# Last group's low parts by TensorE, in two named PSUM banks: an edge-gated graph layer

## The chip, the cores and the metric

The kernel runs on one core of a Trainium2 chip. The time is the device time of one execution in microseconds (us); the kernel before has a median of 1105.02 us over 3 runs (1098.43 to 1110.40). The engines are TensorE (PE, with its weight loads as PEld), VectorE (DVE), ScalarE (ACT), GpSimd (POOL) and SyncE (SP). Each works through its own instructions in order, and semaphores tie them together.

## The reference

The inputs are `x` (16 batches, 1024 nodes, 256 features) and one sparse adjacency matrix `adj` (1024 x 1024, about 9 entries in a row). For every batch, cut to what matters:

```python
pre_u = einsum('bud,dk->buk', h, W1[:d])
pre_v = einsum('bvd,dk->bvk', h, W1[d:])
hidden = relu(pre_u[:, :, None, :] + pre_v[:, None, :, :] + b1)
S = sigmoid(einsum('buvk,ko->buvo', hidden, W2)[..., 0] + b2[0])
a = einsum('buv,bud->bvd', S * A, h)
m = einsum('uv,bud->bvd', A, h) * h
z = beta1*h + beta2*(a @ Wa + ba) + beta3*(m @ Wm + bm)
```

The gate `S` is wanted only where `adj` is not zero, so the kernel works on a list of edges. Each edge (u, v) needs `pre_u` of u, `pre_v` of v, and `h` of u.

## The kernel before, in words

**Blocks, tiles, edges.** The 16 batches make four groups `g` of four. The 1024 receiving nodes make eight blocks `vt` of 128. A step `k` is one block of one group, 32 in all; the last eight (k = 24 to 31) are the last group. A block has ten tiles `n`, two windows of 64 nodes with five tiles each; a tile is 128 edges. Position `s` is a tile's place (0 to 9) in its block.

**Tables.** For each group a table in HBM holds, for each node u, `pre_u` and `h` of the four batches (2048 numbers). Its first half is made by `rows` (line 452), its second is copied. A tile fetches 128 rows of it by an indirect gather (`fetch`, line 515, on POOL) into one of eight `fetched` buffers.

**pre_v as two parts.** `pre_v` plus `b1` of a block is computed by `halves` (line 473) in two halves of 512 columns (two batches each): one matmul puts down the row `b1` (`add_row`, line 448), and `half_product` (line 442) adds the product with `w_v`. The sum is then spread to edges by a 0/1 matrix `mark` in a matmul. That matmul works in the shorter type float32r, so the sum is kept as two numbers: its rounded value, and the low part, which is the sum minus the rounded value. The tile `X` has two windows of 128 rows: in window 0 rows 0 to 63 hold the rounded values of nodes 0 to 63 and rows 64 to 127 their low parts; in window 1 rows 64 to 127 hold the rounded values of nodes 64 to 127 and rows 0 to 63 their low parts. ACT moves the parts there 64 rows at a time. One matmul over 128 rows so adds the rounded value and the low part of 64 nodes. In `halves` ACT casts the product to `X` (line 482) and copies it whole to `low` (line 483), DVE subtracts the rounded value from `low` for both halves at once (line 484), and ACT copies the parts to their places (lines 486 and 489).

**One tile.** `expand` (line 602, PE) makes `pc`, `pre_v` of each edge, in one of two PSUM buffers of 1024 columns. `add` (line 637, DVE) adds it to the fetched `pre_u`. `gate` (line 641) has four DVE instructions that take the relu, multiply by `W2` and sum to a score for each batch, then ACT's sigmoid (line 650) and four ACT instructions that scale the selection matrix `left` (line 652). `aggregate` (line 655, PE) multiplies `left` with the fetched `h` and sums into `acc`.

**One block's end.** ACT copies `acc` to `ev` (`half_end`), PE transposes it in `turn_over` (line 674) into a small PSUM tile, ACT copies that to `LT` (line 685), DVE multiplies by `h` (line 696), and `block_end` (line 701) makes the output product: a bias row, then products with `w_a` and `w_m`, which ACT copies (line 718) and DVE adds to `h` (line 719).

**Banks.** All small products (`pre_v`, transposes, output products, the table's rows) live in a PSUM pool of two banks, handed out in turn by `small` (line 220). A new tile waits until the bank's former tile has been read.

**Order.** The order of the engines' instructions is written out by hand: the loop at line 860 emits, for each tile n, the aggregates of earlier tiles (at odd n, two tiles together), `add(n + 1)`, `gate(n)`, delayed work (`do`), `expand(n + 2)`, and then `products` (line 800). From the tenth tile on, `products` places the work on the block before and the block after by position: transposes at s = 8, 9, 0 and 2, the two halves of the next block's `pre_v` at s = 1 and 3, and the output products at s = 4 to 7. The subtraction of `low` is emitted at s = 5, after the gate, two tiles after the second half; ACT's three moves into `X` come at s = 4, 6 and 7. The first expansion that reads the new `X` is at s = 8.

Of the kernel before, what the change touches and what calls it, by code (L numbers as in the profile page):

```python
# [7 lines left out]
FP = mybir.dt.float32  # L8
FR = mybir.dt.float32r
I32 = mybir.dt.int32  # L10
AF = mybir.ActivationFunctionType
ALU = mybir.AluOpType
AX = mybir.AxisListType
P = 128
# [3 lines left out]
def kernel(  # L18
# [42 lines left out]
    nc = tc.nc  # L61
    B, N, D = x.shape
    NT = N // P
    DC = D // P
    GB = 4
    NG = B // GB
    GD = GB * D
    W = 64
    NW = P // W
# [24 lines left out]
    def load_weights(src, name, engine=nc.scalar):  # L94
        t = const.tile([P, DC, D], FP, name=name)
        engine.dma_start(t, src.rearrange("(c p) k -> p c k", p=P))
        return t
# [3 lines left out]
    def fixed(shape, name, dt=FP):  # L101
        return const.tile(shape, dt, name=name)
# [9 lines left out]
    upto = fixed([P, E], "upto")  # L112
# [3 lines left out]
    row = rows32[:, 0:1]  # L116
# [43 lines left out]
    same = hv.rearrange("p w q one -> p (w q) one").to_broadcast([P, NW * Q, V])  # L160
# [12 lines left out]
    slot_of = fixed([P, NW, TW], "slot_of")  # L173
    for w in range(NW):
        nc.vector.tensor_scalar(slot_of[:, w, :], upto[:, :TW], float(P), row, ALU.mult, ALU.add)
    ident = fixed([P, P], "ident")
    nc.vector.tensor_scalar(ident, upto[:, :P], row, None, ALU.is_equal)
    place = upto[:, :W].rearrange("p (q v) -> p q v", v=V)
    slot, nth = upto, upto[:, :S]

# [11 lines left out]
    b1_p = fixed([P, D], "b1_p", FR)  # L192
# [13 lines left out]
    main = ctx.enter_context(ExitStack())  # L206
    gat = main.enter_context(tc.tile_pool(name="gat", bufs=1))
    one = main.enter_context(tc.tile_pool(name="one", bufs=1))
    big = main.enter_context(tc.tile_pool(name="big", bufs=2))
# [5 lines left out]
    lst = lst.enter_context(tc.tile_pool(name="lst", bufs=1))  # L215
    psc = main.enter_context(tc.tile_pool(name="psc", bufs=2, space=bass.MemoryType.PSUM))
    psa = main.enter_context(tc.tile_pool(name="psa", bufs=1, space=bass.MemoryType.PSUM))
    psm = main.enter_context(tc.tile_pool(name="psm", bufs=2, space=bass.MemoryType.PSUM))

    def small(name):  # L220
        return psm.tile([P, 512], FP, name="misc")


    def aside(vt):
# [177 lines left out]
    def after(step, f):  # L402
        due.setdefault(step, []).append(f)
# [5 lines left out]
    order = [(g, vt) for some in (range(FIRST), range(FIRST, NT)) for g in range(2) for vt in some]  # L409
    again = [(g, vt) for g, vt in order if vt >= FIRST or g == 1]  # L410
    order += [(g, vt) for g in range(2, NG) for vt in range(NT)]
    hTs = {}
# [29 lines left out]
    def half_product(p, hT, wt, h, begun):  # L442
        for bb in range(2):
            for i in range(DC):
                nc.tensor.matmul(p[:, bb * D:(bb + 1) * D], hT[:, 2 * h + bb, i, :], wt[:, i, :],  # L445
                                 start=(i == 0 and not begun), stop=(i == DC - 1), skip_group_check=begun)

    def add_row(p, parts):
        nc.tensor.matmul(p, unit, parts.unsqueeze(1).to_broadcast([P, 2, D]),  # L449
                         start=True, stop=False, skip_group_check=True)  # L450
# [19 lines left out]

    cuts = {}

    def halves(k):
        X = cuts[k] = big.tile([P, NW, GD], FR, name="X")
        low = one.tile([P, GD], FP, name="low")
        for h in range(2):
            step = yield
            c = slice(2 * h * D, (2 * h + 2) * D)
            p = small("p")
            add_row(p, b1_p)  # L480
            half_product(p, hTs[order[k]], w_v, h, True)
            nc.scalar.copy(X[:, 0, c], p)
            nc.scalar.copy(low[:, c], p)  # L483
        after(step + (2 if k else 1), lambda: nc.vector.tensor_tensor(low, low, X[:, 0, :].bitcast(FP), ALU.subtract))  # L484
        yield
        nc.scalar.copy(X[W:, 1, :], X[W:, 0, :].bitcast(FP))
        for w in range(NW):
            yield
            nc.scalar.copy(X[(1 - w) * W:(2 - w) * W, w, :], low[w * W:(w + 1) * W])
# [5 lines left out]
    def do(step):  # L495
        for f in due.pop(step, ()):
            f()

    def go(gen, step):

        try:
            gen.send(step)
        except StopIteration:
            pass

    T = TW * NW

    BS = NG * NT
# [25 lines left out]
    w_v = load_weights(W1[D:2 * D], "w_v", nc.sync)  # L534
# [11 lines left out]
    marks, pcs, accs, evs, hbs, LTs, lefts = {}, {}, {}, {}, {}, {}, {}  # L546
# [12 lines left out]
    parts = halves(0)  # L559
# [76 lines left out]

    def add(n):
        t = fetched[at_slot[n]][:, :GD]
        nc.vector.tensor_tensor(t, t, pcs.pop(n), ALU.add)  # L639

    def gate(n):
        m = len(QUARTERS[n % TW])
# [157 lines left out]
    def products(n, k, s):  # L800
        nonlocal end, parts
        made_rows(n)
        if (s == 2 and 0 < k < BS) or n == total:
            turn_over(k - 1, 1, 1, n)
        z = 3 if n < ROOM else 4
        if z <= s < z + 4 and 0 < k < BS:
            if s == z:
                end = block_end(k - 1)
                next(end)
            go(end, n)  # L810
        if ROOM <= n < total - T:
            if s in (8, 9):
                turn_over(k, 0, s - 8, n)
        elif s == 7 and k < BS:
            turn_over(k, 0, 0, n)
        if s == 7 and k == BS - 1 or s == 8 and n < ROOM:
            turn_over(k, 0, 1, n)
        if (s == 0 and 0 < k < BS) or n == total - 1:
            turn_over(k - (s == 0), 1, 0, n)
        if n == total - 2:  # L820
            end = tail(tails[:2], n)
            next(end)
        elif n == total - 1:
            go(end, n)
        elif n >= total:
            end = tail([tails[2 + n - total]], n)
            next(end)
            go(end, n)
            go(end, n)
        later = n >= ROOM  # L830
        if k + 1 < BS and s - later in (0, 2, 3, 5, 6):
            if s == later:
                parts = halves(k + 1)
                next(parts)
            go(parts, n)

# [22 lines left out]
    done = 0  # L859
    for n in range(total + 2):  # L860
        k, s = divmod(n, T)
        if n < total - 3:
            last_in = n - 1 if n % 2 or n < ROOM else done
        else:
            last_in = n
        while done < min(last_in, total):
            gather_in(done)
            done += 1
        if n % TW == 1 and n // TW + 1 < total // TW:
            load_mark(n // TW + 1)  # L870
        if n < ROOM:
            if n + 2 < total:
                expand(n + 2)
            products(n, k, s)
        if n + 1 < total:
            add(n + 1)
        if n < total:
            gate(n)
            if n + 1 < total:
                left_adj(n + 1)  # L880
        do(n)
        if n >= ROOM and n + 2 < total:
            expand(n + 2)
        if n == 1:
            w_a = load_weights(Wa, "w_a", nc.sync)
            w_m = load_weights(Wm, "w_m", nc.sync)
            bias = load_rows(bm, D, "bias", nc.sync, spare[:, 1])
            ba_b = load_rows(ba, D, "ba_b", nc.sync, spare[:, 2])
            be1 = load_rows(beta1, 1, "be1", nc.sync)
            be2 = load_rows(beta2, 1, "be2", nc.sync)  # L890
            be3 = load_rows(beta3, 1, "be3", nc.sync)
            after(10, scale_late)
        if s in (5, 7) and k < BS - 1:
            h = s // 7
            hb = big.tile([P, 2, D], FP, name="h_blk", bufs=4)
            hbs.setdefault(k, []).append(hb)
            g, vt = order[k]
            nc.sync.dma_start(hb.rearrange("p b d -> p (b d)"),
                              table[g][vt * P:(vt + 1) * P, GD + 2 * h * D:GD + (2 * h + 2) * D])
        if n == total - 6:  # L900
            hbs[BS - 1] = hT_free.pop(0).rearrange("p b c n -> p b (c n)")
            for v, m, f in tails:
                for h, o in tail_rows(x, v, m, f):
                    nc.sync.dma_start(h, o)
        for i in advance.get(n, ()):
            next(made[i], None)
        if n in start_list:
            running.append([made[start_list[n]], True, n])
            piece_of(running[-1], n)
        fill(n, False)  # L910
        if n >= ROOM:
            products(n, k, s)
        if n == LISTS:
            assert not running and all(next(x, None) is None for x in made)
            lists_done()
            more = main.enter_context(tc.tile_pool(name="more", bufs=1))
            hT_free.extend(hT_places(more, MORE, NH))
        if n == 120:
            nc.gpsimd.partition_all_reduce(longest, rest, P, bass_isa.ReduceOp.max)
            after(n + 12, count_rest)  # L920
# [7 lines left out]
    with tc.If(any_left > 0):  # L928
        with ExitStack() as s2:
# [4 lines left out]
            for vt in range(NT):  # L934
# [17 lines left out]
                f = fb.tile([P, 2 * GD], FP, name="fb_f")  # L952
# [37 lines left out]
                for b in range(B):  # L990
# [7 lines left out]
                    for k, w in enumerate((w_m, w_a)):  # L998
                        for c in range(DC):
                            nc.tensor.matmul(pz, lt[:, k, c, :], w[:, c, :],  # L1000
                                             start=(k == 0 and c == 0), stop=(k == 1 and c == DC - 1))
# [34 lines left out]
```

## Time and profile before

| | before |
|---|---|
| median of 3 runs | 1105.02 us |
| profiled execution, its own time | 1101.12 us |
| its span | 1099.3 us |
| PE busy | 1022.2 us (93%) |
| DVE busy | 1025.4 us (93%) |
| ACT busy | 872.5 us (79%) |
| POOL busy | 464.3 us (42%) |
| line 484, DVE, 32 subtractions | 40.0 us, 1248 ns each |

The profile is of one execution; "busy" is the time in which an engine has an instruction at work, and the ends of matmuls are modelled. A group of instructions is a line of the kernel with an engine, an operation and a shape; behind its busy time and mean stands the idle time of that engine just ahead of it, with what ended it. The shares are means over stages. From 200 to 800 us PE is busy for 95 to 98 of each 100 us and DVE for 94 to 98; from 900 to 1050 us DVE is busy all the time and PE for 95 to 98%. The granted clock of TensorE is 1.00 from 400 us up to 1050 us.

### The profile page before, as it was taken

How to read it: one execution, taken by the hardware profiler on the slowest of the kernel's cores; microseconds unless marked ns; L12 is line 12 of the kernel's file. 1: busy time of each engine (PE TensorE's matmuls, PEld its weight loads, DVE VectorE, ACT ScalarE, POOL GpSimd, SP SyncE). 2: the span in 40 equal slices, each digit the busy share in tenths (PEclk: the TensorE clock that was granted, in tenths of full speed). 3: DMA queues.
4: the chain of work that ended last, by engine and by line, in shares of the span. 5: the costliest groups of instructions: out<-in, count | busy, mean ns of one | idle time of the engine just before them, and what ended most of it. 6: DMA issues, size and time to landing. Idle time of an engine off the chain costs nothing.

```text
span 1099.3 us, 23917 instructions
## 1 busy us (share of the span) xinstructions
PE 1022.2 (93%) x7645; PEld 726.5 (66%) x7645; DVE 1025.4 (93%) x3487; ACT 872.5 (79%) x2616; POOL 464.3 (42%) x453
## 2 busy tenths in 40 slices
PE   7777889999899999999999999999999999999986
PEld 6654556776667666676777677767766666666653
DVE  8788888898999999999999999999999999999994
ACT  3347667787778888888988889888889888888873
POOL 2746575445347433563334343433343333333330
PEclk9988989999899999999999999999999999999999
DMA  9999799999999999999999999999999999999991
GB/s 285 331 391 311 295 327 303 356 394 382 384 343 344 391 410 381 384 378 396 408 382 400 406 400 398 386 398 388 353 362 383 372 350 357 359 372 363 354 335 42
DMA packets 149030, 394.54 MB, mean 359 GB/s; under 512 B 18224, under 2 KB 96048, under 8 KB 112688
## 3 DMA queue, kind: packets, MB, share of 16 engines
q0 software_dynamic: 50240, 300.11, 69.6%
q1 hardware_dynamic: 85360, 79.71, 22.9%
q10 hardware_dynamic: 13296, 13.11, 3.6%
q8 instruction: 62, 1.02, 0.3%
q14 instruction: 72, 0.59, 0.1%
HBM read 396.93 MB, written 50.33 MB: 407 GB/s over the span
## 4 chain that ended last, share of the span: by engine, by line
PE 39%; DVE 32%; issue 10%; ACT 9%; DMA 6%; POOL 2%; another core or an unknown queue 0%; SPq 0%; POOLq 0%; DVEq 0%; ACTq 0%
DVE fetched L647 15%; DVE fetched L639 12%; PE acc L664 10%; PE misc L713 10%; PE misc L445 7%; PE pc L607 7%; ACT left L652 3%; PE misc L682 2%; DMA hT<-in_xT_dram 2%; DMA hT<-in_x_dram 2%; PE misc L449 1%; DMA fetched<-table,uidx 1%; DVE low L484 1%; DVE h_blk L719 1%; DVE LT L696 1%
## 5 line engine op out<-in xcount | busy, mean ns | idle before, releaser
L518 POOL DMA_INDIRECT fetched<-table,uidx x320 | 345.5, 1080 | 540.9 <-PE acc L664 384.1
L647 DVE SCALAR_TENSOR_TENSOR fetched<-fetched,w_b 128x256 f32<-128x256 f32 x1280 | 476.5, 418 | 0.0
L639 DVE TENSOR_TENSOR fetched<-fetched,pc 128x1024 f32<-128x1024 f32 x320 | 387.9, 1212 | 38.1 <-PE pc L607 23.1
L652 ACT ACTIVATE left<-left,gt 128x32 f32<-128x32 f32 (+1 forms) x1280 | 299.5, 304 | 10.4
L664 PE MATMUL acc<-fetched,left 128*32 128x256 f32 x4096 | 271.7, 390 | 5.9 <-ACT left L652 4.6
L607 PE MATMUL pc<-X,mark 128*128 128x512 f32 x640 | 245.9, 466 | 12.1 <-DVE fetched L639 12.0
L664 PEld LDWEIGHTS acc<-fetched,left 128*32 128x32 f32 x4096 | 123.7, 111 | 113.1 <-issue 38.8
L650 ACT ACTIVATE gt<-sc,b_b 128x4 f32<-128x4 f32 x320 | 95.5, 298 | 94.8 <-DVE fetched L647 84.4
L607 PEld LDWEIGHTS pc<-X,mark 128*128 128x128 f32 x640 | 106.3, 191 | 91.8 <-issue 48.9
L713 PE MATMUL misc<-w_a,LT 128*128 128x256 f32 x496 | 118.7, 383 | 0.0
L713 PE MATMUL misc<-w_m,LT 128*128 128x256 f32 x496 | 117.2, 379 | 0.0
L445 PE MATMUL misc<-w_v,hT 128*128 128x256 f32 x448 | 108.1, 385 | 1.0 <-DMA hT<-in_xT_dram 1.0
L682 PE MATMUL misc<-ident,ev 128*128 128x128 f32 x512 | 81.3, 282 | 27.0 <-ACT low L483 9.3
L713 PEld LDWEIGHTS misc<-w_a,LT 128*128 128x128 f32 x496 | 94.7, 191 | 15.7 <-issue 0.4
L713 PEld LDWEIGHTS misc<-w_m,LT 128*128 128x128 f32 x496 | 93.9, 189 | 15.2
L617 ACT ACTIVATE left<-onehot,val 128x64 f32<-128x64 bf16 (+1 forms) x320 | 102.9, 322 | 0.0
L385 POOL DMA_INDIRECT val<-in_adjT_dram,vidx x80 | 87.6, 1095 | 33.2 <-issue 18.9
L647 DVE DVE_READ_ACCUMULATOR fetched<-fetched,w_b 128x1 f32 x1280 | 100.4, 78 | 0.0
L682 PEld LDWEIGHTS misc<-ident,ev 128*128 128x128 f32 x512 | 61.2, 143 | 55.1 <-ACT low L483 14.7
L445 PEld LDWEIGHTS misc<-w_v,hT 128*128 128x128 f32 x448 | 86.6, 194 | 16.0 <-DMA hT<-in_xT_dram 1.9
L672 ACT COPY ev<-acc 128x512 f32<-128x512 f32 x128 | 74.7, 584 | 15.4 <-PE acc L664 6.8
L685 ACT COPY LT<-misc 128x512 f32<-128x512 f32 x128 | 73.1, 572 | 5.6 <-PE misc L682 2.9
(178 smaller groups left out, 974.6 us busy)
## 6 DMA issues: line engine op xcount, KB each, us to landing
h_blk<-table SPq DMA_DIRECT2D x62, 256.0 KB
out_dram<-h_blk SPq DMA_DIRECT2D x62, 256.0 KB
hT<-in_xT_dram SPq DMA_DIRECT2D x28, 512.0 KB
table<-in_x_dram ACTq DMA_DIRECT2D x24, 512.0 KB
table<-tab SPq DMA_DIRECT2D x48, 256.0 KB
fetched<-table,uidx POOLq DMA_INDIRECT x320
table<-in_x_dram SPq DMA_DIRECT2D x8, 512.0 KB
table<-fetched SPq DMA_DIRECT2D x8, 512.0 KB
```

The lines of the kernel that those rows point to most:

```text
L385: nc.gpsimd.indirect_dma_start(out=val[:, i, j:j + 1], out_offset=None, in_=adj_flat, in_offset=bass.IndirectOffsetOnAxis(ap=vidx[:, i, j: ...
L445: nc.tensor.matmul(p[:, bb * D:(bb + 1) * D], hT[:, 2 * h + bb, i, :], wt[:, i, :], start=(i == 0 and not begun), stop=(i == DC - 1), skip ...
L518: nc.gpsimd.indirect_dma_start(out=fetched[at_slot[n]], out_offset=None, in_=table[g], in_offset=bass.IndirectOffsetOnAxis(ap=uidx[:, vt * ...
L607: nc.tensor.matmul(pcs[n][:, c], marks[n // TW][:, j * P:(j + 1) * P], cuts[k][:, w, c], start=True, stop=True)
L617: nc.scalar.activation(lefts[n][:, :m, 1::GB, :], onehot[:, i, o:o + m, :].unsqueeze(2).to_broadcast([P, m, GB // 2, V]), AF.Copy, scale=v ...
L639: nc.vector.tensor_tensor(t, t, pcs.pop(n), ALU.add)
L647: nc.vector.scalar_tensor_tensor(t[:, b, :], t[:, b, :], 0.0, w2_b, ALU.max, ALU.mult, accum_out=sc[:, b:b + 1])
L650: nc.scalar.activation(gt, sc, AF.Sigmoid, bias=b2_b)
L652: nc.scalar.activation(lefts[n][:, :m, 2 * b, :], lefts[n][:, :m, 1 + b // 2 * GB, :], AF.Copy, scale=gt[:, b:b + 1])
L664: nc.tensor.matmul(accs[h][b * 2 * V:(b + 1) * 2 * V, r, :], left[:, i, 2 * b - b % 2:2 * b - b % 2 + 2].rearrange("p k v -> p (k v)"), f[ ...
L682: nc.tensor.transpose(pt[:, r, :, c, :], ev[:, r, c * P:(c + 1) * P], ident)
L713: nc.tensor.matmul(pz[:, bb * D:(bb + 1) * D], LTs[k][:, 2 * h + bb, i if bb else 1 - i, c, :], wt[:, c, :], start=False, stop=(i == 0 and ...
```

## The change

In the last group only (`turned(k)`, k of 24 and above), the low part is made by TensorE in PSUM. ACT casts the product with its sign turned, so `X` holds minus the rounded value. A matmul with the identity adds that to the product in its PSUM tile, which is then the low part; ACT copies it out with its sign turned too. As both parts have the sign turned, `add` subtracts `pc` for these blocks. The identity is now declared float32r, with a plain float32 view for the transposes.

A half's PSUM tile now stays in use from its product (s = 1 and 3) until its low part is read (start of s = 4 and 5). So the two banks have names: each call of `small` switches to the other bank, and the second half is put into the bank taken last (`same`), which is that of the transposes at s = 2. The work at s = 4, 6 and 7 of `halves` falls away; the identity matmuls come first at s = 4 and s = 5.

```diff
-    ident = fixed([P, P], "ident")
-    nc.vector.tensor_scalar(ident, upto[:, :P], row, None, ALU.is_equal)
+    ident_r = fixed([P, P], "ident_r", FR)
+    nc.vector.tensor_scalar(ident_r, upto[:, :P], row, None, ALU.is_equal)
+    ident = ident_r.bitcast(FP)
...
-    psm = main.enter_context(tc.tile_pool(name="psm", bufs=2, space=bass.MemoryType.PSUM))
-
-    def small(name):
-        return psm.tile([P, 512], FP, name="misc")
+    psm = main.enter_context(tc.tile_pool(name="psm", bufs=1, space=bass.MemoryType.PSUM))
+    bank = 0
+
+    def small(name, same=False):
+        nonlocal bank
+        bank ^= not same
+        return psm.tile([P, 512], FP, name=f"misc{int(bank)}")
...
+    def turned(k):
+        return k >= NT * (NG - 1)
+
+    def halves_turned(k):
+        X = cuts[k] = big.tile([P, NW, GD], FR, name="X")
+        ps = []
+        for h in range(2):
+            yield
+            c = slice(2 * h * D, (2 * h + 2) * D)
+            p = small("p", h == 1)
+            ps.append(p)
+            add_row(p, b1_p)
+            half_product(p, hTs[order[k]], w_v, h, True)
+            nc.scalar.activation(X[:, 0, c], p, AF.Copy, scale=-1.0)
+            nc.scalar.copy(X[W:, 1, c], X[W:, 0, c].bitcast(FP))
+        for h, p in enumerate(ps):
+            yield
+            c = slice(2 * h * D, (2 * h + 2) * D)
+            nc.tensor.matmul(p, ident_r, X[:, 0, c], start=False, stop=True, skip_group_check=True)
+            for w in range(NW):
+                nc.scalar.activation(X[(1 - w) * W:(2 - w) * W, w, c], p[w * W:(w + 1) * W], AF.Copy, scale=-1.0)
...
-        nc.vector.tensor_tensor(t, t, pcs.pop(n), ALU.add)
+        nc.vector.tensor_tensor(t, t, pcs.pop(n), ALU.subtract if turned(n // T) else ALU.add)
...
-        if k + 1 < BS and s - later in (0, 2, 3, 5, 6):
+        if k + 1 < BS and s - later in ((0, 2) if turned(k + 1) else (0, 2, 3, 5, 6)):
             if s == later:
-                parts = halves(k + 1)
+                parts = (halves_turned if turned(k + 1) else halves)(k + 1)
                 next(parts)
...
+        if s in (4, 5) and turned(k + 1) and k + 1 < BS:
+            go(parts, n)
```

## The prediction

> **What bounds the kernel now.** I read three views: the busy time of each engine in stretches one block long, then the groups of instructions inside that stretch, then the instructions in order of time around one changed place.
>
> First the stretches. Each one below runs from one subtraction of `low` (line 484) to the next, in the last group. Columns: stretch, its length, busy time (instructions) of PE, PEld, DVE, ACT, POOL, the granted clock, DMA share, GB/s.
>
> ```profile
> 838.44:867.29 28.85, 27.65 (x217) 18.99 (x217) 28.85 (x96) 25.71 (x79) 10.18 (x11) 1.00 0.98 380
> ...
> 982.74:1011.62 28.88, 27.69 (x217) 18.99 (x217) 28.88 (x97) 25.73 (x80) 10.19 (x11) 1.00 0.97 358
> ```
>
> DVE is busy for the whole block, 28.85 us of 28.85, and every block takes the same time: DVE sets the pace. But PE is busy for 27.65, so it is only 1.2 us behind. A change that takes work from DVE and gives work or waits to PE must be priced on PE too. The next view, the groups of the same stretches (columns: busy us, mean ns | idle before), gives the prices:
>
> ```profile
> L639 DVE TENSOR_TENSOR fetched<-fetched,pc 128x1024 f32<-128x1024 f32 x70 | 84.5, 1207 | 0.0
> ...
> L489 ACT CAST X<-low 64x1024 fp32r<-64x1024 f32 x14 | 14.6, 1046 | 0.3
> ...
> L484 DVE TENSOR_TENSOR low<-low,X 128x1024 f32<-128x1024 f32 x8 | 9.7, 1214 | 0.0
> ...
> L482 ACT CAST X<-misc 128x512 fp32r<-128x512 f32 x14 | 7.9, 563 | 0.0
> ...
> L449 PE MATMUL misc<-b_p,unit 128*128 128x512 f32 x14 | 5.5, 396 | 0.0
> ```
>
> DVE's subtraction has 0.0 idle before it: nothing covers it. Last, the order of time in one block (start, us, engine, line). PE, at the tiles numbered 3 to 5 of the block:
>
> ```profile
> 917.07 0.40 PE L449 MATMUL misc<-b_p,unit 128*128 128x512 f32 x1
> 917.30 1.89 PE L445 MATMUL misc<-w_v,hT 128*128 128x256 f32 x8
> 918.84 0.81 PE L607 MATMUL pc<-X,mark 128*128 128x512 f32 x2
> 919.49 0.40 PE L449 MATMUL misc<-bias_p,unit 128*128 128x512 f32 x1
> 919.73 1.89 PE L713 MATMUL misc<-w_a,LT 128*128 128x256 f32 x8
> 921.54 1.93 PE L664 MATMUL acc<-fetched,left 128*32 128x256 f32 x32
> 923.41 0.74 PE L607 MATMUL pc<-X,mark 128*128 128x512 f32 x2
> ```
>
> ACT over the same stretch:
>
> ```profile
> 918.29 0.56 ACT L685 COPY LT<-misc 128x512 f32<-128x512 f32 x1
> 919.38 0.30 ACT L650 ACTIVATE gt<-sc,b_b 128x4 f32<-128x4 f32 x1 [0.52 <-DVE fetched L647]
> 919.71 0.96 ACT L652 ACTIVATE left<-left,gt 128x32 f32<-128x32 f32 x4
> 920.58 0.31 ACT L617 ACTIVATE left<-onehot,val 128x32 f32<-128x32 bf16 x1
> 920.79 0.56 ACT L482 CAST X<-misc 128x512 fp32r<-128x512 f32 x1
> 921.25 0.58 ACT L483 COPY low<-misc 128x512 f32<-128x512 f32 x1
> 922.50 0.30 ACT L650 ACTIVATE gt<-sc,b_b 128x4 f32<-128x4 f32 x1 [0.67 <-DVE fetched L647]
> ```
>
> And DVE:
>
> ```profile
> 922.39 1.21 DVE L639 TENSOR_TENSOR fetched<-fetched,pc 128x1024 f32<-128x1024 f32 x1
> ...
> 924.94 1.21 DVE L484 TENSOR_TENSOR low<-low,X 128x1024 f32<-128x1024 f32 x1
> 926.08 1.21 DVE L639 TENSOR_TENSOR fetched<-fetched,pc 128x1024 f32<-128x1024 f32 x1
> ```
>
> The reader is to see who is ahead. The expansion at 923.41 ends at 924.15 and makes the `pc` that DVE adds at 926.08: PE leads DVE by 1.93 us there. ACT stands on DVE's heels: each gate (L650) waits for DVE's scores, and every copy behind it in ACT's order is late with it. PE now runs ahead of ACT: it writes the bias row at 919.49, before ACT has touched the second product of the same tile (920.79).
>
> **The change, part by part.**
>
> *Removed from DVE:* one subtraction a block, eight in all (the last group's blocks; they start at 838.4 to 1040.4). From start to the next start it takes 926.08 - 924.94 = 1.14 us. If nothing else came in its place: 8 x 1.14 = 9.1 us gained, and the block would take 27.72.
>
> *ACT:* before, two casts (0.563), two copies of `low` (0.58) and three 64x1024 casts (1.042 to 1.046) make 5.4 us a block. After: two 128x512 activations and six of 64x512. No row shows 64x512; I take 0.57, since 128x512 takes 0.563 here and the length of a row, not the number of rows, parts 0.563 from 1.04. That makes 1.13 + 3.42 = 4.6. ACT is idle for 3.1 us of each block, so these 0.8 us bring nothing. What counts is where the copies stand. [...]
>
> *Added on PE:* two products with `ident_r`, 128x512, a block. The nearest rows are the bias row (next start 0.23 us later, 919.49 to 919.73) and the expansion (0.57 to 0.65 for a pair and the step to the next). I take 0.23, bounds 0.2 and 0.42. PE's 1.2 us of idle covers 0.46; without that cover it would be 3.7 us.
>
> *The banks.* This is where the time goes. Both banks were taken in turn, so a product found a bank that had been read a tile or more before. Now each half's product stays open until its second product is read, and two takers come at once behind an unread tile. PE works in order, so what stands behind a waiting matmul waits too.
>
> Wait 1, tile 3: the second half's product is put into the bank of the transposes just before it (tile 2), so line 449 must wait for ACT's copy L685, which ends at 918.29 + 0.56 = 918.85. I add 0.05 for the signal: 918.90 in place of 917.07. Its product is then ready 1.83 later, 919.19 + 1.83 = 921.02.
>
> Wait 2, tile 4: the output product (bias row, then `w_a`) takes the bank of the first half. That is free once ACT has done, in its order: the negated cast of the second half (from 921.07; 0.28 late), its copy of 64 rows (from 921.65), and two negated copies of the first half's low part (from 922.25 and 922.72, spaced 0.47 like L482 to L483), ending at 923.28. The bias row starts at 923.33 in place of 919.49: 3.84 us late. Queued behind it on PE are `w_a`, the new second `ident_r` product, 32 aggregates and the expansion that DVE needs: 923.41 + 3.84 + 0.23 = 927.48, done 0.74 later, and DVE adds at 928.26.
>
> Before, that add stood at 926.08, with the subtraction in front of it; without it DVE could start at 924.94. So DVE stands idle for 3.32 us, less the 1.14 it was spared: **2.18 us more a block**. PE doesn't win it back. From that add to the next such place DVE and ACT run as before, each tied to the other, and the release is again counted from DVE's gate. PE gets idle time elsewhere, which is no use. Eight blocks: 8 x 2.18 = 17.4 us.
>
> The bounds: a 64x512 copy costs at least what the shortest cast near it does (128x32, 0.31) and at most 1.04 (64x1024). Three of them stand before the release: from 0.7 us earlier to 1.4 later, so 1.5 to 3.6 us a block, 12 to 29 us. I keep 17, nearest to the 512-long row.
>
> [...] In this trace the rotation shows as PE writing at 919.49 while ACT is still three instructions away. Without any lead of PE, wait 2 alone would make 3.84 x 8 = 31 us; the lead that the rows show brings it down to the 17 above.
>
> *At nothing:* adding turned to subtracting is the same instruction on DVE; the identity keeps its bits; other tiles take the two banks in the same turn as before; the queues of SP and POOL keep their order. Gathers are issued after aggregates, so some come about 2 us later; eight buffers cover it, as DVE has no wait for a transfer in these blocks. Without that cover, a late gather would add straight to DVE.
>
> **The sum.** The profiled execution took 1101.12 us (span 1099.3 and 1.8 around it): 1101.1 + 17.4 = 1118.5. The median of the three runs is 1105.02, 3.9 above it. I forecast from the median: **1122 us**.
>
> **The rivals.**
>
> *A, faster:* PE's lead covers the waits and DVE stays the bound: 1105 - 9.1 = 1096. For it: the lead is 1.9 to 3 us at every tile. It decides at a bias row before 921.15 (no loss) and in full before 920.0. Against it: at 920.79 ACT has only begun the second cast. Chance 0.08; half of it beyond 1%.
>
> *B, PE the bound without bank waits:* 27.66 (the mean of these blocks) + 0.46 = 28.12 a block in place of 28.86, 0.74 x 8 = 5.9: 1099. For it: PE is 96% busy. Against: the wait is in the built order. Chance 0.06.
>
> *C, a wait half as dear:* ACT does the short copies in 0.33, or the first half's copies are ready sooner: 0 to 11 us more, about 1111. Chance 0.10.
>
> *D, dearer:* at tile 5 ACT itself now waits for PE's second `ident_r` product (about 925.8) and holds back the gate behind it. If this reaches the aggregates and then the next expansion, 1 us a block more: 1130. Against: the scores wait there anyway. Chance 0.08.
>
> *That the change doesn't do what it says:* in the built order DVE loses the eight subtractions and PE gets the sixteen products, so this has no share.
>
> **How the numbers follow.** The forecast has 0.68, of which 0.06 ends within 1% (the low end of the bounds, 12 us, with a run that falls low). 1% is about 11 us, what a measurement with runs of 1098 to 1110 can tell from no change. Slower: 0.62 + 0.08 = 0.70. Same: 0.06 + 0.10 + 0.06 + 0.03 = 0.25. Faster: 0.05. The range of 8 in 10 takes in the bounds of the copies and half of C: 1108 to 1131.
>
> **What would show it.** Right: blocks of about 31 us in the last group, DVE busy for about 27.7 of them (89%), PE idle before the bias row with ACT's negated copies as releaser, and DVE idle before its add behind PE. Wrong: blocks under 28.9 us and DVE still without idle time. The prediction fails if ACT finishes the first half's copies by 921, or if PE's lead at tile 7 is larger than 3.3 us when it meets the wait.

## The result, and the profile after

| | before | after |
|---|---|---|
| median, same chip | 1101.72 us (6 runs) | 1138.26 us (6 runs) |
| lowest to highest | 1096.90 to 1110.40 | 1128.75 to 1140.49 |
| profiled execution, its own time | 1101.12 us | 1128.75 us |
| its span | 1099.3 us | 1126.9 us |

The changed kernel is **slower by 3.05%** (ratio 1.0305, 95% interval 1.0243 to 1.0367): 34 to 37 us, where 17 were forecast. The direction is right; the size is half of what came, and the time lies above the range. The profiled execution was the quickest of its six, so it shows less of the loss than the median has.

First the stretches of the last group again, now from DVE's `add` at position 7 of one block to the same place in the next (length, then busy time of PE, PEld, DVE, ACT, POOL, granted clock, DMA share, GB/s):

```profile
846.65:878.14 31.49, 28.07 (x219) 19.20 (x218) 27.85 (x94) 25.30 (x82) 10.05 (x10) 1.00 0.90 345
878.14:910.82 32.68, 29.74 (x219) 20.24 (x218) 27.96 (x95) 25.33 (x82) 10.05 (x10) 0.95 0.83 309
```

DVE, which was busy 28.86 of 28.86, has lost its subtraction (27.85) and now stands idle for 3.6 us of a block of 31.49. There are two kinds of block: six of the eight periods take 31.49 to 31.54, two take 32.68 and 32.74, and in these the granted clock is 0.95 in place of 1.00. The eight together take 254.4 us against 231.1 before: 23.4 us more.

Next the waits in these blocks (engine, what it was about to write, whom it waited for: us in total, times, longest):

```profile
DVE fetched L665 <- PE pc L633: 31.1, 10, 3.7
...
PE misc L453 <- ACT LT L711: 11.8, 7, 1.7
PE misc L453 <- ACT X L497: 11.3, 7, 1.7
```

The last two lines are the two bank waits of the forecast, once a block each: the second half's row `b1` behind the copy of the transposes (wait 1), and the bias row behind the copies of the first half's low part (wait 2). The first line is what DVE feels of them: eight waits of some 3.6 us in this window, and one of about 1.1 in each of the two longer blocks. Now one undisturbed block (its clock stays at 1.00) in order of time, at the same tiles as in the forecast (13.71 us later on this clock). PE:

```profile
930.22 0.73 PE L633 MATMUL pc<-X,mark 128*128 128x512 f32 x2
932.63 0.50 PE L453 MATMUL misc<-b_p,unit 128*128 128x512 f32 x1 [1.68 <-ACT LT L711]
932.97 1.89 PE L449 MATMUL misc<-w_v,hT 128*128 128x256 f32 x8
...
937.29 0.50 PE L453 MATMUL misc<-bias_p,unit 128*128 128x512 f32 x1 [1.74 <-ACT X L497]
937.63 1.89 PE L739 MATMUL misc<-w_a,LT 128*128 128x256 f32 x8
939.17 0.58 PE L495 MATMUL misc<-X,ident_r 128*128 128x512 f32 x1
...
941.54 0.73 PE L633 MATMUL pc<-X,mark 128*128 128x512 f32 x2
```

ACT between the two waits, and then DVE:

```profile
934.90 0.60 ACT L490 ACTIVATE X<-misc 128x512 fp32r<-128x512 f32 x1 [0.30 <-PE misc L449]
935.53 0.61 ACT L491 CAST X<-X 64x512 fp32r<-64x512 f32 x1
936.05 1.19 ACT L497 ACTIVATE X<-misc 64x512 fp32r<-64x512 f32 x2
```

```profile
942.31 1.22 DVE L665 TENSOR_TENSOR fetched<-fetched,pc 128x1024 f32<-128x1024 f32 x1 [3.61 <-PE pc L633]
```

The chain is there to be read: PE waits 1.68 us, its product sets ACT off at 934.90, ACT's four pieces end at 937.24, PE waits 1.74 us for them, and the expansion at 941.54 reaches DVE after 3.61 us of idle time.

So 23.4 us come from the last group. The rest was not foreseen, and lies far ahead of it: in the profile, position 7 of block 20 already comes at 754.15 us, against 749.39 before, and the blocks 1 to 10, in which the edge lists are still being built, are of another length almost one by one. The view of waits of PE over the first 480 us has three lines that name DVE's line 304, a step of the list building (`from`):

```profile
PE misc L708 <- DVE from L304: 8.3, 2, 4.2
...
PE misc L449 <- DVE from L304: 5.9, 1, 5.9
...
PE misc L453 <- DVE from L304: 2.9, 1, 2.9
```

That is 17.1 us. In the kernel before no line of that view names this step.

So there are three questions: what the early loss comes from, what each bank wait costs, and what the clock has to do with it. Times below are medians on one chip for each set of runs, with the kernel before beside them (1102.78 in the first set, 1102.95 in the second, 1102.98 in the third). The sets ran on different chips; differences between sets, such as the 13 and 9 us below, lean on how closely these three agree.

### The profile page after: what moved, and what is told of

The parts are those of the page before. It is cut to its first block, busy times and chain, and to the rows that moved or that the text cites. A ratio compares the mean times of both kernels' runs of the same rounds, so it can differ in the third digit from the quotient of the medians.

```text
span 1126.9 us, 23962 instructions
## 1 busy us (share of the span) xinstructions
PE 1026.0 (91%) x7661; PEld 731.3 (65%) x7661; DVE 1016.5 (90%) x3479; ACT 868.3 (77%) x2624; POOL 463.9 (41%) x453
## 4 chain that ended last, share of the span: by engine, by line
PE 43%; DVE 28%; ACT 13%; issue 8%; DMA 6%; SPq 2%; POOL 0%; DVEq 0%; ACTq 0%; POOLq 0%
DVE fetched L673 14%; PE acc L690 12%; PE misc L739 11%; DVE fetched L665 9%; PE misc L449 8%; PE pc L633 7%; ACT left L678 4%; PE misc L708 2%; DMA table<-in_x_dram 2%; PE misc L453 2%; ACT gt L676 1%; ACT LT L711 1%; DMA table<-tab 1%; DVE h_blk L745 1%; ACT left L643 1%
## 5 line engine op out<-in xcount | busy, mean ns | idle before, releaser
L673 DVE DVE_READ_ACCUMULATOR fetched<-fetched,w_b 128x1 f32 x1280 | 104.1, 81 | 0.0
L708 PE MATMUL misc<-ident_r,ev 128*128 128x128 f32 x512 | 80.2, 280 | 24.7 <-ACT low L509 9.4
L708 PEld LDWEIGHTS misc<-ident_r,ev 128*128 128x128 f32 x512 | 61.8, 143 | 49.1 <-ACT low L509 15.7
```

Of the source, the lines that this page charges most:

```text
L673: nc.vector.scalar_tensor_tensor(t[:, b, :], t[:, b, :], 0.0, w2_b, ALU.max, ALU.mult, accum_out=sc[:, b:b + 1])
L708: nc.tensor.transpose(pt[:, r, :, c, :], ev[:, r, c * P:(c + 1) * P], ident)
```

## The early loss: names, turns, or the identity

**Names only.** No block is turned, so `halves` and the subtraction are as before; what is left of the change is the naming of the banks and the type of the identity.

```diff
     def turned(k):
-        return k >= NT * (NG - 1)
+        return k >= BS
```

> The banks keep their names and the identity its float32r type, but no block is turned: all 32 blocks make their low part as before. Theory (the loss is made by the two waits for a bank in the eight turned blocks, and by the TensorE clock that falls when PE stands in them): the time of the kernel before, 1102 us within its spread. Rival (naming the banks or the new type of the identity slows the first 23 blocks): 1108 us or more, since the profile of the changed kernel is 4 to 5 us late before the first turned block.

Measured 1118.12 us (1111.21 to 1122.58), ratio 1.0158 (1.0097 to 1.0218). The rival held, my theory fell: about 15 us are lost with no turned block at all. The last blocks take 28.85 to 28.87 us, as before; position 7 of block 20 comes at 759.73, 10.3 us late. The waits of PE over the first 480 us show the same step as in the changed kernel:

```profile
PE misc L708 <- DVE from L304: 8.4, 2, 4.3
PE misc L449 <- DVE from L304: 5.9, 1, 5.9
...
PE misc L453 <- DVE from L304: 3.2, 1, 3.2
```

I then compared, tile by tile, which bank the built programs give to the small tiles in their order of use. The kernel before does **not** alternate strictly. Of 331 small tiles, ten get the bank of the tile just ahead of them: numbers 30, 31, 53, 54, 60, 85, 86, 126, 127 and 328. The first nine lie in blocks 1 to 11, next to the products of the list building (lines 289 and 341), whose results DVE reads late. The rotating pool gave the next tile the bank that was free; the names make it take the other one, and wait until DVE has read the list's product.

**The old turns.** Two kernels give these nine tiles their old banks again and change nothing else: one is the changed kernel, the other the kernel with names only.

```diff
-    bank = 0
+    bank = calls = 0
+    STAY = (30, 31, 53, 54, 60, 85, 86, 126, 127)
 
     def small(name, same=False):
-        nonlocal bank
-        bank ^= not same
+        nonlocal bank, calls
+        bank ^= not (same or calls in STAY)
+        calls += 1
```

> Names of banks and the identity's type only, no turned halves, as in the first run, and the nine tiles in their old banks. Theory: 1102, like the kernel before (within 1%, 1096 to 1109), since only the strict turns cost. Rival, the identity as a rounded type slows the transposes, or the names order something else: 1112 or more, as the run with names only (1118).

> The changed kernel whole (turned halves, their two waits, the products with the identity), but nine of the 331 small tiles, all in the first eleven blocks, take again the bank that they had before: the rotating pair did not alternate strictly there (tiles 30, 31, 53, 54, 60, 85, 86, 126 and 127 in order of first use got the bank of the tile ahead of them). Theory: the loss in the early blocks came from strict turns alone, so it is gone: tile 7 of block 20 within 2 us of the kernel before, not 5 to 16 late. What is left is the last group: 8 x 2.63 us for the two waits = 21, and 1.2 to 1.7 for each stretch at half clock, 2 to 8 in all. 1102 + 21 + 2 to 8 = 1125 to 1131. Rival, the early loss has another cause (the identity's type, chance in the order of the lists): the time stays at 1134 to 1142.

With names only: 1105.10 us (1099.01 to 1109.14, 10 runs), ratio 1.0009 (0.9975 to 1.0043), no difference from the kernel before. The naming, and the identity's type, cost nothing by themselves that these runs can tell; the strict turns cost 1118.12 - 1105.10 = 13 us. The changed kernel with the old turns: 1129.25 us (1127.54 to 1132.74), ratio 1.0244 (1.0190 to 1.0298), 9 us below the changed kernel and inside the 1125 to 1131 of its theory. In the profiles of both, no wait of PE for this step of the list building is left. My number for block 20 was too tight: position 7 came 3.1 us later than before, in the names-only kernel 4.35 late. The first ten blocks differ by several us from one execution to another (one block took 46.68 us in a kernel whose median is that of before), so single profiles don't settle a few us there; the medians do.

## What each wait in the last group costs

**Wait 2 taken away.** The last copies read `X` in SBUF, so nothing reads the first half's bank late.

```diff
-nc.scalar.activation(X[...], p[w * W:(w + 1) * W], AF.Copy, scale=-1.0)
+nc.scalar.activation(X[...], X[w * W:(w + 1) * W, 0, c].bitcast(FP), AF.Copy, scale=-1.0)
```

> Left out: the low part itself. The last two copies of each half read X in SBUF in place of the product's bank, so the bank is free once the identity product is done and the output's bias row no longer waits for ACT; the number and size of all instructions stay the same. Theory: wait 2 is gone, wait 1 (second half for the transposes' copy) is left, and costs 0.4 to 0.5 us a block against the kernel before: 29.3 to 29.5 us a block, 1104 to 1110 us. Rival (the new instructions cost the time, not the wait): 31.5 us a block and 1130 us or more.

Measured 1121.35 us (1121.22 to 1125.07), ratio 1.0173 (1.0118 to 1.0228), above the theory's 1104 to 1110. It has the strict turns, so about 13 us of it are the early loss; without them some 1108 would be left. Three of the eight periods take 29.45 to 29.71 us, the five with a fall of the clock 31.09 to 31.49, one of each:

```profile
850.66:882.15 31.49, 29.71 (x220) 20.45 (x219) 28.05 (x95) 25.48 (x81) 10.23 (x11) 0.95 0.91 347
882.15:911.60 29.45, 27.77 (x219) 19.22 (x218) 27.84 (x95) 25.38 (x81) 10.04 (x10) 1.00 0.93 342
```

Against 28.86 before, wait 1 alone costs 0.6 us a block where the clock holds (PE is idle for 1.68 of the 29.45); wait 2 makes the larger part of the 2.63. Where the clock falls, a block without wait 2 is almost as long as one with both waits and no fall.

**Both waits taken away** (the second half's product goes into the other bank, as in the kernel before, and no bank is read late; the copies read `X`):

```diff
-            p = small("p", h == 1)
+            if h == 1:
+                nc.tensor.matmul(ps[0], ident_r, X[:, 0, :2 * D], start=False, stop=True, skip_group_check=True)
+            p = small("p")
...
-            nc.tensor.matmul(p, ident_r, X[:, 0, c], start=False, stop=True, skip_group_check=True)
+            if h == 1:
+                nc.tensor.matmul(p, ident_r, X[:, 0, c], start=False, stop=True, skip_group_check=True)
...
-nc.scalar.activation(X[...], p[w * W:(w + 1) * W], AF.Copy, scale=-1.0)
+nc.scalar.activation(X[...], X[w * W:(w + 1) * W, 0, c].bitcast(FP), AF.Copy, scale=-1.0)
```

> Left out: the low part itself. As the run without wait 2, and the first half's identity product comes just ahead of the second half's product, which then takes the first half's bank; no matmul waits for a bank that ACT has not yet read. All instructions of the change are there. Theory: the work itself is a gain, DVE sets the pace at 27.7 to 28.2 us a block, 1093 to 1099 us. Rival (the work is the cost: PE has no room for the two products, or ACT for the pieces): 29 us a block or more, 1103 us or more.

Measured 1114.11 us (1110.92 to 1122.95), ratio 1.0117 (1.0033 to 1.0201); here too the strict turns are in it. Two periods of the last group:

```profile
883.29:912.09 28.80, 28.74 (x220) 19.51 (x219) 27.85 (x94) 25.05 (x81) 10.40 (x10) 1.00 0.95 354
912.09:941.65 29.56, 29.50 (x223) 20.16 (x222) 27.84 (x94) 25.79 (x82) 11.01 (x11) 1.00 0.95 350
```

PE is busy for all but 0.06 us of each, and the eight periods average 28.7. The theory missed: the blocks are longer than its 27.7 to 28.2, and with 13 us for the strict turns taken off, 1101 us are still more than its 1093 to 1099. It looks like the forecast's rival B (PE the bound), at 28.7 in place of its 28.12. But that PE can't be quicker is not shown. Here are PE's 768 aggregates in six blocks, in this kernel (line 693) and in the version further below with the transposes ahead of the gate (line 688), where a block takes 28.28 (columns: stretch, length, busy PE, PEld, clock, DMA share, GB/s):

```profile
883.29:1056.22 172.93, 55.24 (x768) 25.51 (x768) 1.00 0.96 357
```

```profile
876.20:1045.89 169.69, 49.57 (x768) 24.62 (x768) 1.00 0.97 365
```

The same products keep PE "busy" for 5.7 us less there. In this kernel their weight loads wait for ACT's `left`, which the view of waits of the other does not list:

```profile
PEld acc L693 <- ACT left L681: 4.7, 18, 0.4
```

So a PE that the profile shows busy all the time still holds waits. What sets 28.7 here is not settled beyond that.

**The subtraction put back.** The changed kernel, and on DVE at position 5 one subtraction of 128x1024 on data that nobody uses.

```diff
+        if s == 5 and turned(k + 1) and k + 1 < BS:
+            low = one.tile([P, GD], FP, name="low")
+            after(n, lambda low=low: nc.vector.tensor_tensor(low, ukey, ukey, ALU.subtract))
```

> The changed kernel with a subtraction of 128x1024 on DVE at the place of the old one in each turned block (its result is read by nobody). Theory: DVE stands idle for 3.6 us just behind that place, so 1.14 us more hide there: 31.5 us a block, the time of the changed kernel, 1130 to 1140 us. Rival (what is taken from DVE is still gained, and the loss is bigger than it looks): 9 us more than the changed kernel.

Measured 1140.00 us (1135.25 to 1144.95), ratio 1.0358 (1.0290 to 1.0425); the interval takes in the changed kernel's 1.0305, and the median is 1.7 us above the changed kernel's, where the rival asked for 9. Its undisturbed blocks take 31.48 to 31.55, those of the changed kernel 31.49 to 31.54. What the change spares DVE is idle time in this schedule: it is worth nothing as long as the waits stand.

## The clock

In the changed kernel's slower blocks the granted clock falls for 3.41 us. In the traces of the kernels before and after, every stretch at half clock that ends inside the trace lasts one, two, three or five times 3.41 us, and in each trace they all begin on one regular grid of 3.41 us. The stretches here lie on it to within 0.1 us:

```profile
897.40:900.81 3.41, 1.73 (x9) 1.05 (x7) 3.41 (x14) 2.79 (x10) 0.99 (x1) 1.00 1.00 416
900.81:904.22 3.41, 3.41 (x10) 2.48 (x8) 2.71 (x10) 1.91 (x7) 0.00 (x0) 0.51 1.03 432
962.30:965.71 3.41, 1.73 (x8) 1.42 (x8) 3.41 (x11) 2.82 (x12) 0.74 (x1) 1.00 1.00 411
```

In the first, PE was busy for 1.73 us of 3.41 (0.51), and in the next the clock is half (0.51 on average, as the stretch begins a little early). The `w_v` product in it takes 3.06 us in place of 1.89. The third row has the same 1.73, and its block is one of those of 31.5: half a stretch without work comes ahead of a fall here, but does not always bring one.

**PE kept busy.** The changed kernel with the old turns, and ahead of each wait PE repeats a matmul four times.

```diff
-        for h in range(2):
+        for h in range(2) if not (turned(k + 1) and k + 1 < BS and n % T in (5, 6)) else (0, 0, 0, 0, 0, 1):
```

> The changed kernel with the nine tiles in their old banks, and in the turned blocks the expansions just ahead of the two waits (tiles 5 and 6) repeat their first 128x512 matmul four times, some 0.9 us of PE work inside each of the idle times of 1.7 us, into the tile that they write anyway. Theory, the clock falls because PE stands idle twice in a short time: no half clock in the last group, every block 31.5 or less, 2 to 8 us less than the same kernel without the repeats: 1121 to 1125. Rival, the clock falls for another reason (load over a longer time): blocks of 32.7 stay, the time is the same or, if the repeats come late for DVE, up to 8 x 0.9 = 7 us more.

Measured 1124.63 us (1118.74 to 1132.27), ratio 1.0212 (1.0138 to 1.0287). In its one profile the theory holds: no half clock in the last group's eight periods, all of them 31.48 to 31.54 us, with eight matmuls more in each. The next fall comes at 1079.03, in the last block, where nothing is repeated. The same kernel without the repeats had three periods of 32.5 to 33.2. One of each:

```profile
904.03:935.52 31.49, 29.93 (x227) 20.68 (x226) 27.93 (x94) 25.33 (x82) 10.03 (x10) 1.00 0.87 325
```

```profile
845.02:877.96 32.94, 29.75 (x219) 20.35 (x218) 27.95 (x95) 25.30 (x81) 10.06 (x10) 0.95 0.86 330
```

More work on PE, and a shorter block than those with a fall. In the times the difference is 4.6 us in the expected direction, but the intervals overlap: the profiles, one of each kernel, show it, the times alone don't. Over the profiles of the turned blocks in which the clock fell, I laid the grid of 3.41 us over PE's matmuls: the share of the stretch just ahead of a fall was 0.51 in each (13 falls, in four kernels). The kernel with the repeats has no stretch below 0.76, the one with only wait 1 left, below, none under 0.57, and neither had a fall there. But 0.51 is no threshold. The stretches of 0.49, which hold wait 2, brought no fall in any of the three kernels that have them (the first row below, of the changed kernel), and in the kernel before the clock fell at 290.2 us after a stretch in which PE was busy for 0.63 (the other two rows):

```profile
839.40:842.81 3.41, 1.68 (x8) 1.11 (x7) 3.41 (x16) 3.31 (x10) 0.00 (x0) 1.00 0.97 406
```

```profile
286.79:290.20 3.41, 2.14 (x16) 1.74 (x14) 3.41 (x11) 3.07 (x10) 1.23 (x1) 1.00 1.04 418
290.20:293.61 3.41, 1.87 (x13) 1.11 (x16) 3.41 (x11) 2.74 (x12) 0.00 (x0) 0.51 1.03 421
```

That filling the idle times kept the clock up is shown, in one profile; what decides between two such stretches stays open.

## Other places for the same work

**The first half read early.** With the old turns, the first half's product with the identity is emitted at position 3, ahead of the second half's product; its bank is then free long before the output product.

```diff
-        ps = []
...
-            ps.append(p)
...
-        for h, p in enumerate(ps):
             yield
...
-        if s in (4, 5) and turned(k + 1) and k + 1 < BS:
+        if s in (3, 5) and turned(k + 1) and k + 1 < BS:
             go(parts, n)
```

(The second condition stands behind the loop over `gather_in`, not ahead of it.)

> The nine tiles in their old banks and only the first half's product with the identity read early (tile 3); the transposes of tile 2 stay behind the gate, so the second half's bank is still the one of the transposes just ahead. Theory: wait 2 is gone and wait 1 stays: about 29.5 us a block (as the undisturbed blocks of the run without the second read, 29.49) in place of 28.28 with both moves, 9 blocks at 1.2 more than that run: 1097 + 11 = 1104 to 1112, more if the clock falls. Rival, the early read alone frees PE's lead enough: 28.3 a block, 1094 to 1100.

Measured 1107.33 us (1102.24 to 1115.02, 10 runs), ratio 1.0068 (1.0033 to 1.0104), as the theory had it. Wait 2 is gone, wait 1 is left, 29.28 to 29.37 us a block:

```profile
866.13:895.48 29.35, 27.91 (x219) 19.32 (x218) 27.86 (x94) 25.27 (x81) 10.41 (x11) 1.00 0.93 345
```

```profile
PE misc L455 <- ACT LT L709: 10.1, 7, 1.5
DVE fetched L663 <- PE pc L631: 9.3, 7, 1.4
```

PE waits up to 1.5 us for the copy of the transposes, and hands 1.4 on to DVE. The block is 0.5 us longer than before.

**And the transposes ahead of the gate.** On top of it, the transposes of position 2 are issued at the top of the step, ahead of the gate's instructions on ACT, so that ACT copies them earlier.

```diff
+        if s == 2 and turned(k + 1) and k + 1 < BS:
+            turn_over(k - 1, 1, 1, n)
...
-        if (s == 2 and 0 < k < BS) or n == total:
+        if (s == 2 and 0 < k < BS and not (turned(k + 1) and k + 1 < BS)) or n == total:
```

> The nine tiles in their old banks, and the turned halves put elsewhere: the first half's product with the identity is read as soon as it is made (tile 3, not after the second half's product), and the transposes of tile 2 are issued ahead of the gate. Each bank is then released before its next taker comes, so both waits should shrink to under 0.5 us. Theory: PE is the bound at 28.1 to 28.8 us a block (PE was busy 28.1 and more a block in the run without waits), so 1096 to 1104, no gain that can be told from the kernel before, though DVE has 8 x 1.14 = 9 us less to do. Rival A: the early read makes PE wait for ACT's cast of 128x512 in line, 0.6 to 1.2 us a block: 1107 to 1112. Rival B: DVE is the bound and the gain comes out in full: 1093.

Measured **1097.03 us** (1093.82 to 1108.17, 10 runs), ratio 0.9956 (0.9929 to 0.9982): inside the theory's range, and below both kernels. Against the one before it is a gain of 0.4%, small, by an interval that just leaves out 1.

```profile
904.48:932.76 28.28, 27.78 (x219) 19.23 (x218) 27.87 (x94) 25.24 (x81) 10.52 (x11) 1.00 0.96 359
```

A block takes 28.28 us against 28.86 before and 29.35 with wait 1. PE is busy 27.78, DVE 27.87: both are within half a us of the whole, and neither fills it. So the same arithmetic on the same engines loses 2.63 us a block or gains 0.58, by where two reads of a bank stand.

**The subtraction on POOL.** The kernel before, with the last group's eight subtractions on POOL, which is idle for two thirds of a block (busy for 10.2 us of 28.86).

```diff
-lambda: nc.vector.tensor_tensor(low, low, X[:, 0, :].bitcast(FP), ALU.subtract)
+lambda: (nc.gpsimd if k >= NT * (NG - 1) else nc.vector).tensor_tensor(low, low, X[:, 0, :].bitcast(FP), ALU.subtract)
```

> The kernel before, with the eight subtractions of low in the last group given to POOL in place of DVE and nothing else: no bank waits, no added PE work. DVE has 1.14 us less in each block, and PE (27.66 busy) is the bound. Theory: 28.0 to 28.3 a block in place of 28.86, 5 to 7 us less in all: 1096 to 1098. Rival, POOL's subtraction takes so long beside DVE (they slow each other, or a gather issued behind it comes late) that the blocks are longer: 29 to 31 a block, 1104 to 1120.

Measured 1129.61 us (1123.91 to 1136.25), ratio 1.0259 (1.0213 to 1.0306). The rival held: most blocks take 30.6 us. POOL, and DVE at the same time:

```profile
911.04 2.37 POOL L484 TENSOR_TENSOR low<-low,X 128x1024 f32<-128x1024 f32 x1
```

```profile
910.02 0.46 DVE L647 SCALAR_TENSOR_TENSOR fetched<-fetched,w_b 128x256 f32<-128x256 f32 x1
...
910.41 3.29 DVE L647 SCALAR_TENSOR_TENSOR fetched<-fetched,w_b 128x256 f32<-128x256 f32 x1
```

An instruction of 0.42 us on DVE takes 3.29 and ends at 913.70, 0.29 behind POOL's. DVE is spared 1.14 us and pays 2.87, at seven of the eight subtractions (3.28 to 3.30 us each). That is only a part of the loss: six periods of 30.6 make 10 us, and a single one of 40.35, the first with a subtraction on POOL, makes 11.5. There POOL stands idle for 11.77 us ahead of its subtraction, without an engine that it waits for ("issue"), and the expansion behind it comes late:

```profile
853.73 2.33 POOL L484 TENSOR_TENSOR low<-low,X 128x1024 f32<-128x1024 f32 x1 [11.77 <-issue]
```

```profile
857.19 1.22 PE L607 MATMUL pc<-X,mark 128*128 128x512 f32 x2 [8.74 <-ACT X L489]
```

At the start of this idle time (842.0) the trace has two instructions MODIFY_POOL_CONFIG of line 484, which the other seven subtractions don't have. That they are the reason was not tested.

## Why the prediction was right or wrong

**Right.** DVE was the bound, and its subtraction gives nothing while a wait takes its place (put back, it costs nothing). Both bank waits are where they were forecast, and the steps hold one by one on the common clock: the row `b1` at 918.92 (forecast 918.90), the cast at 921.19 (921.07), the copies done at 923.53 (923.28), the bias row at 923.58 (923.33), the expansion at 927.83 (927.48), DVE's add at 928.60 (928.26). Rival A is out: PE's lead did not cover the waits. Rival C is out: the short copies took 0.59, not 0.33. Rival D's wait exists (ACT stands 1.08 us before the second pair of copies, 939.78), but reaches no expansion: the undisturbed blocks need no such term.

**Wrong, the step that failed:** "At nothing: [...] other tiles take the two banks in the same turn as before". They don't. Nine tiles in the early blocks, which had taken the bank of the tile just ahead of them, now took the other one, and PE waited for the list building. Put at nothing, it costs 13 us between the two names-only kernels, 9 between the two changed ones. With the old turns the changed kernel is 26 us above the kernel before, at 1129.25 and so inside the forecast's 1108 to 1131: this one term carries the result out of the range. I had looked only at the stretch that the change names; the naming is for the whole kernel.

**Left out of the sum:** the clock. The waits make PE idle for half a stretch of 3.41 us, and a fall adds 1.0 to 1.7 us to its block: 2.4 us in the profile of the changed kernel, 4.1 in the one with the old turns.

**Mis-sized:** the waits themselves, 2.63 us a block in place of 2.18, 3.6 us in eight. The pieces of ACT took 0.59 to 0.61 where 0.56 and 0.57 stood, and behind an idle PE the step from the bias row to its product was 0.34, not 0.23; that makes 0.34. The remaining 0.1 is that DVE's own work fell to 27.85, not to 27.72. The 0.05 for the signal, for which the forecast gives no row, came out at 0.06 and 0.05: from ACT's ends at 932.57 and 937.24 to the bias rows at 932.63 and 937.29.

Together, an estimate from these runs: 21 for the waits, 2 to 4 for the clock, 9 to 13 for the turns, 32 to 38 in all, against 34 to 37 measured. That the direction came out right owes nothing to the term that failed: the waits alone are 21 of it, and they were forecast.

## What to carry to other kernels

When a change replaces how buffers are handed out, compare the buffer of every tile in the built order, over the whole kernel, and not only where the change wants something from it: a rotating pool need not rotate strictly (here ten of 331 tiles stayed in the bank of the tile ahead, and strict turns for nine of them cost 9 to 13 us). What an open PSUM bank cost in these runs hung on where its later read stood in the reading engine's order: put the read, or what it waits for, ahead of that engine's next batch of work and the cost can turn into a gain (here from 2.63 us a block lost to 0.58 gained). Where a change gives PE idle time, look at its clock too (here a fall added 1.0 to 1.7 us to its block).

## What was not expected of the hardware

The granted clock fell to half for 3.41 us after a stretch of 3.41 us in which PE was busy for 0.51, with no single idle time longer than 1.74 us in the changed kernel's blocks, and matmuls of no use in these idle times kept it up in the profile (31.5 us a block in place of 32.5 to 33.2). And POOL and DVE did not work side by side here: while POOL subtracted for 2.37 us, a DVE instruction of 0.42 us took 3.29, and so at seven of the eight subtractions (3.28 to 3.30). By the profile DVE's instruction starts 0.63 us ahead of POOL's, long enough to be done by then, and is still the one that is held up; the profiler's spans on POOL are rough. What holds it up was not shown.
